# The end of a two-layer graph network on one core: another order of work for the last pair, written out on three engines

## The chip, the core and the metric

The kernel runs on one core of a Trainium2 chip. The core has a matrix engine (TensorE, PE in the profile, with its weight loads as PEld), a vector engine (VectorE, DVE), an activation engine (ScalarE, ACT), GpSimd (POOL) and SyncE (SP). Each engine runs its own queue of instructions in order, and the queues meet through semaphores. Matrix products go to PSUM, eight banks of 128 x 512 float32, and are read from there by ACT or DVE. Data comes from and goes to the device's memory (HBM) by DMA, issued here from the queues of SP and POOL.

The metric is the device time in microseconds (us), the median of several executions. Before the change it is 2423.75 us (three runs, 2422.8 to 2425.18).

## The reference

Input x has 64 batch elements of 256 nodes and 512 features; adj is a 0/1 matrix of 256 x 256. All is float32.

```python
q, k, v = ((x @ W + b) for W, b in ((Wq, bq), (Wk, bk), (Wv, bv)))    # 8 heads of 64
scores  = q @ k.T / sqrt(64) + (1 - adj) * -1e9
out     = softmax(scores) @ v @ Wo + bo
x       = layernorm(x + out)                         # layer 0
x       = layernorm(x + (adj @ x) @ weight + bias)   # layer 1
```

## The kernel before

**Pairs.** Batch elements are worked on two at a time: pair p of 32 has elements b = 0 and 1, each with two chunks of 128 nodes. Attention is done in two halves of four heads, g = 0 and 1 ("first" and "second" scores and values). The last pair is 31 (p in the code), the one before it 30 (q).

**Products.** Every large product runs as three float32r matmuls on digits of both factors: a high part (a scaled copy on ACT), a low part and a difference (two scalar_tensor_tensor on DVE, lines 268 and 269; for q and k lines 350 to 354). `product` (line 312) is one *block*: 12 matmuls of 128 x 512 (line 318) into one PSUM bank, then one evacuation. Blocks are named by their weights: "v", "q", "k", "o" (attention's output) and "l" (layer 1); four of each per pair, j = 2b + c. Digits of activations live in a pool of four buffers per name: "sh", "sl", "sd" or "high", "low", "diff". Blocks "o" and "l" are evacuated by DVE (line 325), which adds the residual r and sums each row.

**Attention.** `scores` (line 402) takes eight banks in a row and gives 48 matmuls (line 415) and eight exps on ACT (line 419) into the tiles e. `masked` multiplies e by the transposed adjacency matrix, `summed` adds the two halves of the keys (lines 424, 429, DVE). `values` (line 363) forms the sums by 16 matmuls (line 371), copied to zc by ACT (line 373), and the values by 64 small matmuls (line 381), copied to vc (line 385). DVE inverts the sums and multiplies (lines 388 to 400): O. `o_high` and `o_rest` make O's digits.

**Norms.** `with_bo` and `with_b1` add a bias to r (DVE, line 438). A norm over two chunks is `mean` (DVE, line 450), `squared` for each chunk (ACT, line 457, with the sum of squares), `inverse` (DVE line 462, then a pow on POOL, line 463), `less` (DVE, line 468) and `normed` for each chunk (ACT, line 474). After the second layer `normed` also issues the output's DMA on SP; for pair 31 that is one DMA for each chunk (line 477). `normed` of chunk 3 issues the load of r two pairs on (`load_r`, line 82), which waits until the output of the pair that held the buffer is written.

**Layer 1.** `hl_high` (ACT, line 486) and `hl_low` (DVE, line 491) split the normed x, `adj_x` (line 493) multiplies by the adjacency matrix (8 matmuls, line 501) and makes the digits of the result (ACT, then DVE).

**Order.** Functions are called in the order in which their instructions stand on PE, DVE and ACT: `first(w)` and `second(w)` do one pair's attention together with the layers of the pair before (`with tc.manual_schedule`, line 614). For the end, `last()` (line 583), only TensorE's order is as written (line 623); there the order on DVE and ACT comes from a scheduler. POOL and SP are the scheduler's in both. Weights pass through a ring of two stages of three tiles; `stage_end` issues the load of the stage after next on POOL's queue. Weights "o" and "l" of pair 30 stay in the ring for pair 31.

## Time and profile before

| | |
|---|---|
| median of the runs | 2423.75 us |
| profiled execution | 2424.03 us, its span 2422.3 us |
| one pair in the steady part | 73.8 us |
| pair 30's last o block ends | 2342.4 us |
| last matmul of a block ends | 2410.8 us |
| last norm on ACT ends | 2416.25 us |

Times in the tables of the profile are from the span's start. A row of the timeline has the start, the duration from the first start to the last end, the engine, the source line, the operation, what it writes and reads, the shapes and how many instructions it stands for; in brackets, if the engine was idle before, how long and what released it. A row of the table of stages has the stretch, its length, then for PE, PEld, DVE, ACT and POOL the busy time and the number of instructions, the clock granted to TensorE (1.00 is full speed), the share of the DMA engines' time and GB/s. The chain that ended last is followed back from the last instruction to what released each step.

### The profile page before, as it was taken

Reading aid. Unit: us, or ns where it says so; the run is one execution under the profiler, and the core shown is the slowest. Engines: PE = TensorE matmul, PEld = TensorE weight load, DVE = VectorE, ACT = ScalarE, POOL = GpSimd, SP = SyncE. Lnnn points to the kernel's source line nnn. Section 1 sums busy time; section 2 is a strip of 40 time slices with the busy share of each in tenths; the row PEclk is TensorE's granted clock in tenths of the full one; section 3 lists DMA queues with packets and bytes.
Section 4 is the critical chain, followed back from the end, with each engine's and each line's share of the span. In section 5 each row is a group of like instructions: output and inputs, shape, how many; then the busy total and the mean of one; then the engine's idle time right before and its main releaser. Section 6 shows DMA issues by size and latency. Waiting matters only on the chain.

```text
span 2422.3 us, 42885 instructions
## 1 busy us (share of the span) xinstructions
PE 2388.0 (99%) x16894; PEld 1914.0 (79%) x16894; DVE 2002.6 (83%) x3311; ACT 1503.2 (62%) x2796; POOL 448.8 (19%) x735
## 2 busy tenths in 40 slices
PE   8999999999999999999999999999999999999997
PEld 5778878888878888788888788887788787888876
DVE  7888888888888888888988888888889888888865
ACT  5566665665665666656656656666566566566554
POOL 1111121122121211211121212212111112112110
PEclk9999999999999999999999999999999999999998
DMA  8767787777897787877778977778877779777651
GB/s 260 269 221 268 256 278 260 239 239 260 254 306 242 227 268 256 266 270 243 235 261 251 305 249 225 261 258 261 281 239 237 264 251 293 255 229 252 247 191 37
DMA packets 370719, 603.45 MB, mean 249 GB/s; under 512 B 272848, under 2 KB 275152, under 8 KB 310224
## 3 DMA queue, kind: packets, MB, share of 16 engines
q0 software_dynamic: 67824, 493.91, 55.3%
q1 hardware_dynamic: 300576, 104.64, 20.2%
q8 instruction: 135, 2.21, 0.4%
q10 hardware_dynamic: 2112, 2.10, 0.2%
q14 instruction: 72, 0.59, 0.1%
HBM read 551.29 MB, written 49.28 MB: 248 GB/s over the span
## 4 chain that ended last, share of the span: by engine, by line
PE 91%; DVE 3%; ACT 1%; DMA 1%; issue 0%; POOL 0%; POOLq 0%; DVEq 0%; ACTq 0%; SPq 0%
PE ps L318 68%; PE ps L381 8%; PE ps L415 7%; PE ps L501 5%; PE ps L371 2%; DMA r<-in_x_dram 1%; ACT r L474 0%; DVE e L424 0%; DVE hl L491 0%; DVE wr L128 0%; ACT waste L457 0%; DVE sl L268 0%; DVE wr L127 0%; DVE r L438 0%; DVE r L325 0%
## 5 line engine op out<-in xcount | busy, mean ns | idle before, releaser
L424 DVE TENSOR_TENSOR e<-e,adjT 128x1024 f32<-128x1024 f32 x256 | 304.5, 1221 | 1.2 <-ACT e L419 1.2
L318 PE MATMUL ps<-wr,sl 128*128 128x512 f32 x1024 | 278.0, 393 | 6.2 <-ACT wr L131 3.9
L318 PE MATMUL ps<-wr,sh 128*128 128x512 f32 x1024 | 276.3, 391 | 0.0
L318 PE MATMUL ps<-wr,sd 128*128 128x512 f32 x1024 | 275.6, 391 | 0.0
L318 PE MATMUL ps<-low,wr 128*128 128x512 f32 x992 | 271.4, 395 | 0.0
L318 PE MATMUL ps<-high,wr 128*128 128x512 f32 x992 | 266.5, 390 | 0.0
L318 PE MATMUL ps<-diff,wr 128*128 128x512 f32 x992 | 265.0, 389 | 0.0
L419 ACT ACTIVATE e<-ps 128x512 f32<-128x512 f32 x512 | 256.8, 628 | 8.1 <-PE ps L415 8.1
L457 ACT ACTIVATE waste<-r,ln 128x512 bf16<-128x512 f32 x256 | 183.9, 719 | 106.4 <-DVE ln L450 104.2
L381 PE MATMUL ps<-e,v 128*32 128x256 f32 x4096 | 232.9, 379 | 1.2 <-ACT v L329 1.2
L474 ACT ACTIVATE r<-r,ln 128x512 f32<-128x512 f32 x256 | 194.8, 808 | 58.3 <-DMA x<-in_x_dram 31.4
L463 POOL TENSOR_TENSOR ln<-ln,power 128x2 f32<-128x2 f32 x128 | 152.3, 1190 | 412.4 <-DVE ln L462 353.8
L318 PEld LDWEIGHTS ps<-wr,sl 128*128 128x128 f32 x1024 | 191.2, 189 | 46.4 <-ACT wr L131 4.7
L318 PEld LDWEIGHTS ps<-wr,sh 128*128 128x128 f32 x1024 | 193.7, 189 | 41.0
L318 PEld LDWEIGHTS ps<-wr,sd 128*128 128x128 f32 x1024 | 193.3, 189 | 40.6
L318 PEld LDWEIGHTS ps<-high,wr 128*128 128x128 f32 x992 | 186.2, 188 | 41.1
L318 PEld LDWEIGHTS ps<-diff,wr 128*128 128x128 f32 x992 | 186.2, 188 | 39.1
L415 PEld LDWEIGHTS ps<-qT,kT 64*128 64x128 f32 x3056 | 188.9, 188 | 31.4 <-ACT vc L385 14.8
L338 ACT ACTIVATE uncut<-ps,bq 128x512 f32<-128x512 f32 x126 | 86.8, 689 | 199.7 <-PE ps L318 142.9
L350 DVE SCALAR_TENSOR_TENSOR qT<-qT,uncut 128x512 fp32r<-128x512 f32 x126 | 86.7, 688 | 148.2 <-ACT qT L343 148.2
L415 PE MATMUL ps<-qT,kT 64*128 64x256 f32 x3056 | 203.6, 286 | 3.9 <-ACT vc L385 3.1
L318 PEld LDWEIGHTS ps<-low,wr 128*128 128x128 f32 x992 | 177.9, 188 | 35.1 <-issue 0.5
(111 smaller groups left out, 4212.1 us busy)
## 6 DMA issues: line engine op xcount, KB each, us to landing
wr<-qk POOLq DMA_DIRECT2D x183, 1024.0 KB, 7.5
wr<-v POOLq DMA_DIRECT2D x93, 1024.0 KB, 6.7
wr<-o POOLq DMA_DIRECT2D x90, 1024.0 KB, 8.1
wr<-l POOLq DMA_DIRECT2D x90, 1024.0 KB, 8.4
r<-in_x_dram SPq DMA_DIRECT2D x32, 1024.0 KB
out_dram<-r SPq DMA_DIRECT2D x62, 512.0 KB
x<-in_x_dram SPq DMA_DIRECT2D x488, 64.0 KB
qk<-wr POOLq DMA_DIRECT2D x6, 1024.0 KB, 8.4
```

What stands on the lines that cost most here:

```text
L318: nc.tensor.matmul(pm, *pairs[k][i], start=i == 0 and k == 0, stop=i == n - 1 and k == DC - 1)
L338: nc.scalar.activation(to, pm, AF.Identity, bias=bias[:, j:j + 1], scale=scale)
L350: nc.vector.scalar_tensor_tensor(low, high.bitcast(F32), -RHO, UNCUT.pop((name, p, j)), op0=OP.mult, op1=OP.add)
L371: nc.tensor.matmul(at[h * 32:(h + 1) * 32, b, :], ones, sm[:, h % 2, h // 2, :], start=True, stop=True)
L381: nc.tensor.matmul(at[h * 32:(h + 1) * 32, a, :], V[p, b][:, kc, col:col + 32], E[p, g, b, kc][:, h % 2, h // 2, :], start=kc == 0, stop=k ...
L415: nc.tensor.matmul(sc[s][:, a, :], K[p, g][r, a, i, keys], Q[p, g][r, a, i, b * N:(b + 1) * N], start=i == digits[0], stop=i == digits[-1])
L419: nc.scalar.activation(e[:, s], sc[s], AF.Exp, scale=(RHO if (p, g) != (0, 0) else 1.0) * qscale)
L424: nc.vector.tensor_tensor(e, e, mask[:, kc:kc + 1, :].to_broadcast([P, 4, N]), op=OP.mult)
L457: nc.scalar.activation(waste, R[p][b][:, c], AF.Square, bias=t[0][:, c:c + 1], accum_out=t[1][:, c:c + 1])
L463: nc.gpsimd.tensor_tensor(t[2], t[1], power, op=OP.pow)
L474: nc.scalar.activation(r, r, AF.Identity, scale=t[2][:, c:c + 1], bias=t[3][:, c:c + 1])
L501: nc.tensor.matmul(pm[:, j, :], t[:, i, mc, j * P:(j + 1) * P], adjT[:, mc, :], start=mc == 0 and i == 0, stop=mc == NC - 1 and i == 1)
```

## The change

`last()` and the last call of `first` are replaced by `ending()`, which writes the order of pair 31's part on PE, DVE and ACT.

- The second scores of pair 31 no longer stand directly behind its first values, but two o blocks of pair 30 later. Attention of pair 31 stands ahead of the rest of pair 30's layer 1 and of pair 31's o blocks.
- The bias of pair 31's r is added (`with_bo`) behind the digits of the "k" blocks.
- For the second scores of pair 31 each e is two tiles of half the size, in buffers that x and the digits of x had ("x", "high", "low", "diff"); mask and sum work on the halves, each as two instructions in place of one. O of the second half goes to "xT". All digits of pair 31's activations go to "high", "low", "diff".
- `mean`, `inverse` and `less` take a range of chunks. The last norm is done chunk by chunk, so that each of its chunks is squared, inverted and normed by itself.

The computation and the number of matmuls are the same. The order of POOL's and SP's transfers is the same; on POOL there is one pow more.

```diff
--- before.py
+++ after.py
@@ -276,8 +276,7 @@
 
     def set_high(name, p, b, half, a):
 
-        free = p == NP - 1 and (name, half) != ("o", 0) and (name, b) != ("l", 1)
-        names = ("high", "low", "diff") if free else ("sh", "sl", "sd")
+        names = ("high", "low", "diff") if p == NP - 1 else ("sh", "sl", "sd")
         t = SET[name, p, b, half] = [four.tile([P, 2, N], F32R, name=n) for n in names]
         nc.scalar.activation(t[0], a, AF.Copy, scale=CUT)
 
@@ -379,7 +378,7 @@
                     for h in range(4):
                         col = g * HF + h * HD + a * 32
                         nc.tensor.matmul(at[h * 32:(h + 1) * 32, a, :], V[p, b][:, kc, col:col + 32],
-                                         E[p, g, b, kc][:, h % 2, h // 2, :], start=kc == 0, stop=kc == NC - 1)
+                                         E[p, g, b, kc][0][h % 2][:, h // 2, :], start=kc == 0, stop=kc == NC - 1)
             do(between[b])
             vc.append(two.tile([P, 2, N], F32, name="vc"))
             nc.scalar.activation(vc[b], at, AF.Copy)
@@ -396,7 +395,7 @@
         total = acc.rearrange("p b j -> p (b j)")
         nc.gpsimd.tensor_tensor(total, total, seen, op=OP.add)
         for b in range(2):
-            O[p, b, g] = two.tile([P, 2, N], F32, name="o")
+            O[p, b, g] = two.tile([P, 2, N], F32, name="o" if (p, g) != (NP - 1, 1) else "xT")
             nc.vector.tensor_tensor(O[p, b, g], vc[b], rs[:, b, None].to_broadcast([P, 2, N]), op=OP.mult)
 
     def scores(p, g):
@@ -414,19 +413,32 @@
                             r = slice(s * HD, (s + 1) * HD)
                             nc.tensor.matmul(sc[s][:, a, :], K[p, g][r, a, i, keys], Q[p, g][r, a, i, b * N:(b + 1) * N],
                                              start=i == digits[0], stop=i == digits[-1])
-                e = E[p, g, b, kc] = one.tile([P, 2, 2, N], F32, name=f"e{2 * b + kc}")
+                if (p, g) == (NP - 1, 1):
+
+                    names = (("x", two), ("high", four), ("low", four), ("diff", four))
+                    name, pool_of = names[2 * b + kc]
+                    e = [pool_of.tile([P, 2, N], F32, name=name) for _ in range(2)]
+                    whole = []
+                else:
+                    e = one.tile([P, 2, 2, N], F32, name=f"e{2 * b + kc}")
+                    whole, e = [e.rearrange("p s a n -> p (s a) n")], [e[:, s] for s in range(2)]
+                E[p, g, b, kc] = e, whole
                 for s in range(2):
-                    nc.scalar.activation(e[:, s], sc[s], AF.Exp, scale=(RHO if (p, g) != (0, 0) else 1.0) * qscale)
+                    nc.scalar.activation(e[s], sc[s], AF.Exp, scale=(RHO if (p, g) != (0, 0) else 1.0) * qscale)
 
     def masked(p, g, b, kc):
         if 0 <= p < NP:
-            e = E[p, g, b, kc].rearrange("p s a n -> p (s a) n")
-            nc.vector.tensor_tensor(e, e, mask[:, kc:kc + 1, :].to_broadcast([P, 4, N]), op=OP.mult)
+            halves, whole = E[p, g, b, kc]
+            for e in whole or halves:
+                nc.vector.tensor_tensor(e, e, mask[:, kc:kc + 1, :].to_broadcast([P, e.shape[1], N]), op=OP.mult)
 
     def summed(p, g, b):
         if 0 <= p < NP:
             sm = SM[p, g, b] = two.tile([P, 2, 2, N], F32, name="sm")
-            nc.vector.tensor_tensor(sm, E[p, g, b, 0], E[p, g, b, 1], op=OP.add)
+            (h0, w0), (h1, w1) = (E[p, g, b, kc] for kc in range(NC))
+            to = [sm.rearrange("p s a n -> p (s a) n")] if w0 else [sm[:, s] for s in range(2)]
+            for t, e0, e1 in zip(to, w0 or h0, w1 or h1):
+                nc.vector.tensor_tensor(t, e0, e1, op=OP.add)
 
     def masks(p, g, b):
         return [(masked, p, g, b, 0), (masked, p, g, b, 1), (summed, p, g, b)]
@@ -443,11 +455,12 @@
     def with_b1(p, b):
         biased(p, b, b1_s)
 
-    def mean(p, name, b):
-        if 0 <= p < NP:
-            ln = small.tile([P, 4, 2], F32, name="ln")
-            t = LN[p, name, b] = [ln[:, i] for i in range(4)]
-            nc.vector.tensor_scalar(t[0], ST.pop((p, name, b)), -1 / D, None, op0=OP.mult)
+    def mean(p, name, b, cs=slice(0, 2)):
+        if 0 <= p < NP:
+            if cs.start == 0:
+                ln = small.tile([P, 4, 2], F32, name="ln")
+                LN[p, name, b] = [ln[:, i] for i in range(4)]
+            nc.vector.tensor_scalar(LN[p, name, b][0][:, cs], ST[p, name, b][:, cs], -1 / D, None, op0=OP.mult)
 
     def squared(p, name, j):
         if 0 <= p < NP:
@@ -456,15 +469,15 @@
             waste = one.tile([P, D], mybir.dt.bfloat16, name="waste")
             nc.scalar.activation(waste, R[p][b][:, c], AF.Square, bias=t[0][:, c:c + 1], accum_out=t[1][:, c:c + 1])
 
-    def inverse(p, name, b):
-        if 0 <= p < NP:
-            t = LN[p, name, b]
+    def inverse(p, name, b, cs=slice(0, 2)):
+        if 0 <= p < NP:
+            t = [u[:, cs] for u in LN[p, name, b]]
             nc.vector.tensor_scalar(t[1], t[1], 1 / D, EPS, op0=OP.mult, op1=OP.add)
-            nc.gpsimd.tensor_tensor(t[2], t[1], power, op=OP.pow)
-
-    def less(p, name, b):
-        if 0 <= p < NP:
-            t = LN[p, name, b]
+            nc.gpsimd.tensor_tensor(t[2], t[1], power[:, cs], op=OP.pow)
+
+    def less(p, name, b, cs=slice(0, 2)):
+        if 0 <= p < NP:
+            t = [u[:, cs] for u in LN[p, name, b]]
             nc.vector.tensor_tensor(t[3], t[0], t[2], op=OP.mult)
 
     def normed(p, name, j):
@@ -580,35 +593,49 @@
            (block, "q", 1, 1), (k_low, 1, 0), qk0[4:6], (o_high, 0, 0, 0), (o_high, 0, 1, 0), (o_rest, 0, 0, 0),
            (block, "k", 1, 1), qk0[6:], (stage_end, 0), (k_low, 1, 1), (o_rest, 0, 1, 0))
 
-    def last():
+    def ending():
 
         p, q = NP - 1, NP - 2
-        values(p, 0, ([(squared, q, "o", 2), (hl_low, q, 0, 0), (hl_low, q, 0, 1)], [(squared, q, "o", 3)]))
+        c0, c1 = slice(0, 1), slice(1, 2)
+        values(q, 1, ([(squared, q - 1, "l", 2)], [(squared, q - 1, "l", 3)]))
+        scores(p, 0)
+        do((inverse, q - 1, "l", 1), masks(p, 0, 0),
+           (o_high, q, 0, 1), (o_high, q, 1, 1), (block, "v", p, 0), (o_rest, q, 0, 1), (o_rest, q, 1, 1),
+           (less, q - 1, "l", 1), masks(p, 0, 1), (normed, q - 1, "l", 0), (normed, q - 1, "l", 1),
+           (block, "v", p, 1), (normed, q - 1, "l", 2), (normed, q - 1, "l", 3),
+           (with_bo, q, 0), (with_bo, q, 1),
+           (block, "v", p, 2), (block, "v", p, 3), (stage_end, p),
+           (block, "q", p, 2), (qk_high, "q", p, 2), (qk_rest, "q", p, 2),
+           (block, "k", p, 2), (qk_high, "k", p, 2), (qk_rest, "k", p, 2), (with_bo, p, 0),
+           (block, "q", p, 3), (k_low, p, 2), (qk_high, "q", p, 3), (qk_rest, "q", p, 3),
+           (block, "k", p, 3), (stage_end, p), (qk_high, "k", p, 3), (qk_rest, "k", p, 3), (k_low, p, 3), (with_bo, p, 1))
+        values(p, 0)
+        do((block, "o", q, 0), (o_high, p, 0, 0), (o_high, p, 1, 0),
+           (block, "o", q, 1), (mean, q, "o", 0), (squared, q, "o", 0), (squared, q, "o", 1), (inverse, q, "o", 0))
         scores(p, 1)
-        do((inverse, q, "o", 1), (with_b1, q, 0), (less, q, "o", 1),
-           (normed, q, "o", 2), (normed, q, "o", 3), (adj_x, q, 0, 0), (adj_x, q, 0, 1),
-           masks(p, 1, 0), (hl_high, q, 1, 0), (hl_high, q, 1, 1), (hl_low, q, 1, 0), (hl_low, q, 1, 1), (with_b1, q, 1),
-           (block, "l", q, 0), masks(p, 1, 1), (block, "l", q, 1),
-           (adj_x, q, 1, 0), (adj_x, q, 1, 1),
-           (mean, q, "l", 0), (squared, q, "l", 0), (squared, q, "l", 1), (inverse, q, "l", 0),
-           (o_high, p, 0, 0), (o_rest, p, 0, 0), (o_high, p, 1, 0), (o_rest, p, 1, 0))
-        values(p, 1)
-        do((less, q, "l", 0), (o_high, p, 0, 1), (o_rest, p, 0, 1), (o_high, p, 1, 1), (o_rest, p, 1, 1),
-           (block, "l", q, 2), (normed, q, "l", 0), (normed, q, "l", 1), (with_bo, p, 0),
-           (block, "o", p, 0), (with_bo, p, 1), (block, "o", p, 1), (mean, p, "o", 0), (squared, p, "o", 0), (squared, p, "o", 1),
-           (inverse, p, "o", 0), (less, p, "o", 0), (normed, p, "o", 0), (normed, p, "o", 1),
-           (block, "o", p, 2), (hl_high, p, 0, 0), (hl_high, p, 0, 1), (hl_low, p, 0, 0), (hl_low, p, 0, 1),
-           (block, "o", p, 3), (mean, p, "o", 1), (squared, p, "o", 2), (squared, p, "o", 3), (inverse, p, "o", 1), (less, p, "o", 1),
-           (normed, p, "o", 2), (normed, p, "o", 3),
-           (block, "l", q, 3), (mean, q, "l", 1), (adj_x, p, 0, 0), (adj_x, p, 0, 1),
-           (hl_high, p, 1, 0), (hl_high, p, 1, 1), (hl_low, p, 1, 0), (hl_low, p, 1, 1), (with_b1, p, 0), (with_b1, p, 1),
-           (squared, q, "l", 2), (squared, q, "l", 3), (inverse, q, "l", 1), (less, q, "l", 1),
-           (block, "l", p, 0), (adj_x, p, 1, 0), (adj_x, p, 1, 1), (block, "l", p, 1),
-           (normed, q, "l", 2), (normed, q, "l", 3),
-           (mean, p, "l", 0), (squared, p, "l", 0), (squared, p, "l", 1), (inverse, p, "l", 0), (less, p, "l", 0),
-           (block, "l", p, 2), (normed, p, "l", 0), (normed, p, "l", 1), (block, "l", p, 3), (mean, p, "l", 1),
-           (squared, p, "l", 2), (squared, p, "l", 3), (inverse, p, "l", 1), (less, p, "l", 1),
-           (normed, p, "l", 2), (normed, p, "l", 3))
+        do((less, q, "o", 0), masks(p, 1, 0), (normed, q, "o", 0), (normed, q, "o", 1), masks(p, 1, 1)[:1],
+           (block, "o", q, 2), (hl_high, q, 0, 0), (hl_high, q, 0, 1), (hl_low, q, 0, 0), (hl_low, q, 0, 1), masks(p, 1, 1)[1:],
+           (block, "o", q, 3), (stage_end, q), (mean, q, "o", 1), (squared, q, "o", 2), (squared, q, "o", 3),
+           (inverse, q, "o", 1), (adj_x, q, 0, 0), (less, q, "o", 1), (adj_x, q, 0, 1))
+        values(p, 1, ([(normed, q, "o", 2), (normed, q, "o", 3)], [(hl_high, q, 1, 0), (hl_high, q, 1, 1)]))
+        do((o_high, p, 0, 1), (o_high, p, 1, 1), (hl_low, q, 1, 0), (hl_low, q, 1, 1), (o_rest, p, 0, 1), (o_rest, p, 0, 0),
+           (with_b1, q, 0), (block, "l", q, 0), (block, "l", q, 1), (mean, q, "l", 0), (adj_x, q, 1, 0), (adj_x, q, 1, 1),
+           (squared, q, "l", 0), (squared, q, "l", 1), (inverse, q, "l", 0),
+           (block, "o", p, 0), (block, "o", p, 1), (mean, p, "o", 0), (squared, p, "o", 0), (squared, p, "o", 1),
+           (o_rest, p, 1, 1), (inverse, p, "o", 0), (o_rest, p, 1, 0), (less, p, "o", 0), (with_b1, q, 1),
+           (block, "l", q, 2), (normed, p, "o", 0), (normed, p, "o", 1), (hl_high, p, 0, 0), (hl_high, p, 0, 1),
+           (block, "o", p, 2), (hl_low, p, 0, 0), (hl_low, p, 0, 1), (less, q, "l", 0), (normed, q, "l", 0),
+           (block, "o", p, 3), (mean, p, "o", 1), (squared, p, "o", 2), (squared, p, "o", 3), (inverse, p, "o", 1),
+           (adj_x, p, 0, 0), (less, p, "o", 1), (adj_x, p, 0, 1), (normed, p, "o", 2), (normed, p, "o", 3),
+           (hl_high, p, 1, 0), (hl_high, p, 1, 1), (block, "l", q, 3), (hl_low, p, 1, 0), (hl_low, p, 1, 1), (mean, q, "l", 1), (with_b1, p, 0),
+           (block, "l", p, 0), (adj_x, p, 1, 0), (adj_x, p, 1, 1), (normed, q, "l", 1), (squared, q, "l", 2), (squared, q, "l", 3), (inverse, q, "l", 1),
+           (with_b1, p, 1),
+           (block, "l", p, 1), (mean, p, "l", 0), (less, q, "l", 1), (squared, p, "l", 0), (squared, p, "l", 1), (normed, q, "l", 2),
+           (inverse, p, "l", 0), (normed, q, "l", 3),
+           (block, "l", p, 2), (mean, p, "l", 1, c0), (less, p, "l", 0), (squared, p, "l", 2), (normed, p, "l", 0), (normed, p, "l", 1),
+           (inverse, p, "l", 1, c0),
+           (block, "l", p, 3), (mean, p, "l", 1, c1), (less, p, "l", 1, c0), (squared, p, "l", 3), (inverse, p, "l", 1, c1),
+           (normed, p, "l", 2), (less, p, "l", 1, c1), (normed, p, "l", 3))
 
     PE, DVE, ACT = mybir.EngineType.PE, mybir.EngineType.DVE, mybir.EngineType.Activation
     with tc.manual_schedule(engines={PE, DVE, ACT}):
@@ -616,12 +643,10 @@
         first(1, steps_of("o", 0))
         second(1, steps_of("l", 0))
         load_r(1)
-        for w in range(2, NP):
+        for w in range(2, NP - 1):
             first(w)
-            if w < NP - 1:
-                second(w)
-    with tc.manual_schedule(engines={PE}):
-        last()
+            second(w)
+        ending()
 
     good = one.tile([P, 2, N // 32], F32, name="z")
     nc.vector.tensor_scalar(good, acc, RANGE, None, op0=OP.is_le)
```

## The prediction

> **What bounds the kernel now.** I read the page first: span, busy shares, then the chain that ended last.
>
> ```profile
> span 2422.3 us, 42885 instructions
> PE 2388.0 (99%) x16894; PEld 1914.0 (79%) x16894; DVE 2002.6 (83%) x3311; ACT 1503.2 (62%) x2796; POOL 448.8 (19%) x735
> ...
> PE 91%; DVE 3%; ACT 1%; DMA 1%; issue 0%; POOL 0%; POOLq 0%; DVEq 0%; ACTq 0%; SPq 0%
> ```
>
> TensorE is the bound over the whole. In the chain in order of time a pair takes 2269.74 - 2195.92 = 73.8 us, with TensorE never waiting. The steady part is written as before, so only the end can move. The timeline of TensorE alone, from 2340 us on, shows where it waits there (last bracket: idle time and releaser):
>
> ```profile
> 2350.09 0.38 PE L415 MATMUL ps<-qT,kT 64*128 64x256 f32 x1 [0.74 <-ACT vc L385]
> 2352.84 1.65 PE L415 MATMUL ps<-qT,kT 64*128 64x256 f32 x11 [2.37 <-ACT vc L385]
> ...
> 2359.90 1.22 PE L318 MATMUL ps<-wr,sl 128*128 128x512 f32 x2 [1.70 <-DVE sl L268]
> 2361.70 1.22 PE L318 MATMUL ps<-wr,sl 128*128 128x512 f32 x2 [0.58 <-DVE sl L268]
> ...
> 2379.77 0.73 PE L318 MATMUL ps<-wr,low 128*128 128x512 f32 x2 [0.92 <-DVE low L268]
> ...
> 2396.03 0.73 PE L318 MATMUL ps<-wr,low 128*128 128x512 f32 x2 [0.94 <-DVE low L268]
> ...
> 2398.19 0.73 PE L318 MATMUL ps<-wr,low 128*128 128x512 f32 x2 [1.43 <-DVE low L268]
> ```
>
> These waits sum to 8.7 us. The first two are the second scores of pair 31, which stand directly behind its first values and want banks that ACT has not emptied. Then the table of stages (its PEclk is the granted clock):
>
> ```profile
> 2350.00:2353.00 3.00, 0.54 (x3) 0.34 (x3) 1.98 (x7) 1.54 (x4) 1.07 (x3) 0.93 0.00 0
> 2353.00:2356.00 3.00, 3.00 (x18) 2.78 (x19) 2.02 (x3) 3.00 (x7) 0.00 (x0) 0.50 0.00 0
> ...
> 2363.00:2366.00 3.00, 3.00 (x8) 2.35 (x8) 2.12 (x2) 0.00 (x0) 0.00 (x0) 0.50 0.00 0
> 2366.00:2369.00 3.00, 3.00 (x14) 2.39 (x14) 1.84 (x3) 0.00 (x0) 0.00 (x0) 0.96 0.00 0
> ```
>
> After 3.1 us idle within 3.5, the clock is at half for 13.3 us (2352.8 to 2366.1). Less the 2.3 idle in them, half of 11 is lost: 5.5 us. The 2.37 us idle within 3.1 at 2395 left it at 1.00.
>
> So of the 68.4 us from 2342.4 (end of pair 30's o blocks) to the last matmul at 2410.8, 14.2 are waits and half clock. The work itself: 12 blocks of 2.72 (12 matmuls; starts 2.72 apart), values twice 4.54, scores 3.07, eight adj_x at 0.99 = 52.7. Behind the last matmul:
>
> ```profile
> 2414.73 1.52 ACT L474 ACTIVATE r<-r,ln 128x512 f32<-128x512 f32 x2 [1.26 <-DVE ln L468]
> ```
>
> That ends at 2416.25, and the output's transfer takes 6.05 us more to the span's end.
>
> **The change part by part.** I walk the written order over three engines with starts taken apart: ACT exp 0.50, square with its read 0.85, norm 0.76 to 0.80, high copies 0.57 to 0.65; DVE 512-wide two-input 0.60 to 0.65, 1024-wide 1.2, an evacuation (L325) 0.65; handovers 0.03 between DVE and ACT, 0.24 behind TensorE. "v", "q", "k" blocks of pair 31 stay up to 2331.5.
>
> *Attention ahead of the rest.* The bias add of pair 31 moves behind the digits of k block 2. It waits for r in both kernels, landing at 2332.7 (chain: 12.41 from 2320.28). Behind it on DVE stand the digits of q3 and k3: 2334.0 to 2336.6, then ACT's k low to 2337.3, and behind that zc and both vc to 2339.0. Cover: TensorE does values(31,0) 2331.5 to 2336.05 and o blocks 0 and 1 of pair 30 to 2341.5. The scores start there, 4.2 us after k is ready; that slack is the price of a later r. O is out of DVE at 2340.9, the two evacuations at 2342.5. The scores' first banks are free by 2339 and the last pair of banks at 2342.5, wanted at 2343.8: the 3.1 us wait and its half clock go, 8.6 with the 5.5.
>
> *What is late next.* ACT does the two squares of pair 30 (to 2344.4) before the exps, so the first exp frees a bank at 2345.05 against 2344.56: 0.55 wait for o block 2. Exps end 2348.4, norms 2350, hl_high 2351.2. DVE runs 2345.5 to 2354.7 unbroken: 12 half masks and sums, two hl_low, an evacuation. hl_low is done at 2351.65 where o block 3 ended 2350.55: 1.15 wait. The sums of the mask end 2354.7 where adj_x ended 2353.65: 1.1. Then values to 2359.2; l block 0 waits 0.4 for its second low (ACT's squares to 2357.35 hold back adj_x's copies, and DVE waits with them).
>
> *Behind the second values.* DVE is unbroken 2357.9 to 2372.8: O to 2363.85, hl_low 2365.1, o_rest of b0 2367.6, bias 2368.75, evacuations, rests. TensorE runs l 0, 1, adj_x, o31 0, 1, l 2 without wait to 2375.15. o31 block 2 needs o_rest(31,1,0), written behind the norm's inverse, which waits for squares ending 2376.1: low at 2376.9, a wait of 1.85. o31 3 ends 2382.45, adj_x 2384.4, l30 3 2387.15, l31 0 waits 0.45 (rest at 2388), adj_x, l31 1 2394.95, l31 2 2397.7, l31 3 2400.4.
>
> *The sum on TensorE.* 2342.4 + 52.7 + waits 5.5 (0.55 + 1.15 + 1.1 + 0.4 + 1.85 + 0.45) = 2400.6, the walk says 2400.4: 10.4 us sooner.
>
> *Norms by chunk.* Removed: one square and one norm behind the last evacuation, 0.85 + 0.76. Added: one mean, inverse, less on DVE (0.17 each), one pow on POOL. But ACT comes to the end late: with_b1 and a DVE wait for the squares of l30 put l31 1's evacuation at 2397.6, its squares at 2397.85 to 2399.55, pair 30's last norms to 2401.1, chunk 0's mean waits for those, square 2402.25, two norms 2403.8, square of chunk 1 2404.7, pow 2405.65, norm 2405.9 to 2406.7. So the tail from the last matmul is 6.3 instead of 5.5: 0.8 is given back. A pow of one column is in no row: between 0.22 (add of 16 columns, L395) and 1.59; I take 0.69, the commonest row of the same operation.
>
> *At nothing.* Halved masks: 12 halves are 7.2 to 7.7 against six whole at 1.2 = 7.2; I take 7.2, upper end +0.5. The exps' new tiles last held x and x's digits, read until 2331.5, ten us before. SP issues the same transfers in the same order, POOL's weight loads keep their places; the last outputs (1.5 MB from 2401.1 to 2406.7) would need 270 GB/s where the page's slices reach 320: 0 to +0.5.
>
> [...] POOL's pow took 0.69 with DVE idle and 1.59 at 2400.16 with the bias add (1.23) beside it. The written order puts DVE work beside most of the last pows, but there the less has 0.6 to 1.2 of other DVE work ahead of it. [...]
>
> Span: 2422.3 - 10.4 + 0.8 = 2412.7. The profiled execution took 2424.03, 1.73 outside its span and 0.28 above the runs' median of 2423.75: 2412.7 + 1.73 - 0.28 = 2414.2, 0.4% faster.
>
> **The rivals.**
>
> *The clock gate trips.* TensorE's waits of 1.15 and 1.1 stand 1.95 us apart; at most 1.55 idle fall in any 3.5 us, where 2.37 did nothing and 3.1 did. Against it stands that margin, for it that hand-walked waits grow. Price: 4.4 us at half (the recovery at 2361.7 to 2366.1 took that) costs 2.2, a full 13 us costs 5.5: 2416.4 to 2419.7. [...]
>
> *Better: the waits don't come.* Without them the last matmul is at 2395.1, and with 9.9 of tail (11.5 less 1.6) the time is 2406.5. Against: DVE has some 51 us of work in the 61 between O and the last evacuation, and each wait above has a named DVE or ACT item.
>
> *Slower: the squares stand in the path.* DVE and ACT now keep a written order, so at each of the eight norms from 2342 on what is behind the pair of squares waits out 1.73 us (rows of L462: idle 1.73, releaser ACT waste). If nothing hid them, that is 13.8 us; the walk charges TensorE 0.55, 0.4, 1.85 and 0.45 of it. The other 10.6 would give 2424.8, slower than before by 1; past 2428.6 only with half a us more behind each. It decides from 9.6 us of added wait. For it: DVE has 51 us of work (16 evacuations, 12 mask halves and sums, 8 hl_low, 8 rests of adj_x, 4 of o, 4 biases, two O, the small steps) in the 63.5 from 2339.6 to 2403.1. Against: at pair 30's l norms and the first o norm of 31, other DVE work is written into the wait.
>
> **How the numbers follow.** The walk, within 3 to 4 us of its sum: 0.68. Clock gate: 0.13. Better: 0.04. Squares in the path, with most of the gain gone: 0.09 inside 0.2% of before, 0.06 slower. About 0.2% (4.8 us) is what a measurement tells from no change; the limit is 2418.9, which about a sixth of the gate's case exceeds (0.02). Faster 0.68 + 0.11 + 0.04 = 0.83, same 0.09 + 0.02 = 0.11, slower 0.06. Range: the walk's 2410.5 below, and above to 2420.5 to take in the gate's 5.5 and the ends of the unknown costs (0.5 + 0.5 + 0.9).
>
> **What would show it.** Right: scores(31,1) without a wait at their start, granted clock 1.00 through 2350 to 2400, last matmul near 2400, o31 block 2 waiting some 2 us for DVE low, last norm at 2406 to 2407. Wrong: clock at 0.50 near 2355, an ACT wait at the first scores (r landing late), or a tail over 13 us.

## The result, and the profile after

The changed kernel takes 2413.28 us (median of five runs, 2412.33 to 2414.19), against 2422.95 us for the kernel before on the same chip (five runs, three of them those of the section on the time before). The ratio is 0.9957, 95% interval 0.9946 to 0.9968: 0.4% faster, 9.7 us. The prediction was 2414.2. Three of the later kernels (the second scores back, the second values late, the l blocks early) each had one slow execution of 3994 to 13675 us, which the ratios leave out and which moves their medians by 0.2 us at most.

The profiled execution took 2412.73 us, its span is 2411.0. From the page of the changed kernel, the span, the busy shares and the shares of the chain that ended last:

```profile
span 2411.0 us, 42905 instructions
PE 2382.0 (99%) x16894; PEld 1908.6 (79%) x16894; DVE 2003.9 (83%) x3320; ACT 1504.1 (62%) x2796; POOL 449.5 (19%) x736
...
PE 91%; DVE 3%; ACT 1%; DMA 1%; issue 0%; POOL 0%; POOLq 0%; DVEq 0%; ACTq 0%; SPq 0%
```

The matmuls are the same 16894 and TensorE is still the bound; its busy time fell by 6.0 us, about what the half clock cost, and the rest of the gain is idle time. Single profiles differ by up to 1.8 us in when the end of the kernel is reached (pair 30's second sums start between 2300.84 and 2302.67 in all the profiles of this study, whatever the end looks like). So I compare ends by their **length**: from the start of those sums to the matmul that counts, the last one on TensorE. Before: 2410.77 - 2302.09 = 108.68 us. After: 2399.94 - 2301.16 = 98.78. The change shortens it by 9.9; another 0.93 of the 11.3 between the two spans lies ahead of the change.

The timeline of TensorE in the changed kernel, with the rows that answer to those of before: the second scores, every wait, the sums of the second values, and the count.

```profile
2330.67 1.07 PE L370 MATMUL ps<-sm,ones 128*32 128x256 f32 x16
...
2340.83 3.14 PE L414 MATMUL ps<-qT,kT 64*128 64x256 f32 x48
2344.29 1.20 PE L317 MATMUL ps<-wr,sl 128*128 128x512 f32 x4 [0.32 <-ACT x L427]
...
2351.03 1.99 PE L514 MATMUL ps<-adjT,hl 128*128 128x256 f32 x15 [0.87 <-DVE hl L504]
2352.95 1.50 PE L370 MATMUL ps<-sm,ones 128*32 128x256 f32 x13
...
2359.14 0.73 PE L317 MATMUL ps<-wr,sl 128*128 128x512 f32 x2 [0.35 <-DVE sl L268]
...
2376.38 1.17 PE L317 MATMUL ps<-wr,low 128*128 128x512 f32 x4 [1.72 <-DVE low L268]
...
2387.37 0.73 PE L317 MATMUL ps<-wr,low 128*128 128x512 f32 x2 [0.20 <-DVE low L268]
...
2399.94 0.22 PE L656 MATMUL ps<-table,ones 128*32 128x1 f32 x2
```

The scores run without a wait. The waits in brackets sum to 3.46 us, where before had 8.68. One more is not in brackets: 13 of the sums take 1.50 us where 16 took 1.07 at 2330.67, and sums and values together take 5.10 (2352.95 to 2358.05) where the first ones took 4.45 (2330.67 to 2335.12). That is the wait for the mask's sums, about 0.6. The table of stages (after the busy times, the granted clock of TensorE) for the two longest waits:

```profile
2350.00:2353.00 3.00, 2.13 (x21) 1.85 (x23) 3.00 (x7) 0.24 (x1) 0.00 (x0) 1.00 0.03 5
2353.00:2356.00 3.00, 3.00 (x47) 1.44 (x50) 1.76 (x5) 1.14 (x3) 0.00 (x0) 1.00 0.00 0
...
2373.00:2376.00 3.00, 1.66 (x8) 1.04 (x6) 2.47 (x7) 1.63 (x4) 0.34 (x2) 1.00 0.00 0
2376.00:2379.00 3.00, 2.62 (x12) 2.20 (x13) 2.83 (x6) 1.91 (x3) 0.78 (x1) 1.00 0.00 0
```

The granted clock is 1.00 from 2325 us to 2404.58, 4.6 us behind the last matmul. The end on ScalarE:

```profile
2402.60 0.71 ACT L470 ACTIVATE waste<-r,ln 128x512 bf16<-128x512 f32 x1
...
2403.30 0.80 ACT L487 ACTIVATE r<-r,ln 128x512 f32<-128x512 f32 x1
2404.51 0.81 ACT L487 ACTIVATE r<-r,ln 128x512 f32<-128x512 f32 x1 [0.40 <-DVE ln L481]
```

The last norm ends at 2405.32, 5.4 us behind the last matmul (5.5 before), and the output takes 5.7 us more (6.05 before).

### The profile page after: what moved, and what is told of

Its sections match the earlier page's. It is cut to its first block, busy times and chain, and to the rows that moved or that the text cites. A ratio compares the mean times of both kernels' runs of the same rounds, so it can differ in the third digit from the quotient of the medians.

```text
span 2411.0 us, 42905 instructions
## 1 busy us (share of the span) xinstructions
PE 2382.0 (99%) x16894; PEld 1908.6 (79%) x16894; DVE 2003.9 (83%) x3320; ACT 1504.1 (62%) x2796; POOL 449.5 (19%) x736
## 4 chain that ended last, share of the span: by engine, by line
PE 91%; DVE 3%; ACT 1%; DMA 1%; issue 0%; POOL 0%; POOLq 0%; DVEq 0%; ACTq 0%; SPq 0%
PE ps L317 68%; PE ps L380 8%; PE ps L414 8%; PE ps L514 5%; PE ps L370 2%; DMA r<-in_x_dram 1%; ACT r L487 0%; ACT waste L470 0%; DVE r L324 0%; DVE wr L128 0%; DVE hl L504 0%; DVE low L268 0%; DVE wr L127 0%; DVE sm L441 0%; DVE r L450 0%
## 5 line engine op out<-in xcount | busy, mean ns | idle before, releaser
L317 PE MATMUL ps<-wr,sl 128*128 128x512 f32 x1008 | 271.6, 391 | 4.6 <-ACT wr L131 3.9
L317 PE MATMUL ps<-wr,sh 128*128 128x512 f32 x1008 | 270.6, 390 | 0.0
L317 PE MATMUL ps<-wr,sd 128*128 128x512 f32 x1008 | 269.7, 389 | 0.0
L414 PEld LDWEIGHTS ps<-qT,kT 64*128 64x128 f32 x3056 | 188.1, 187 | 27.8 <-PE ps L380 12.3
L114 POOL DMA_DIRECT2D wr<-qk x183 | 98.5, 539 | 564.4 <-PE ps L317 564.3
```

The costliest lines, as they stand in the source:

```text
L114: nc.gpsimd.dma_start(W[stage][i], SCRATCH[name, i])
L317: nc.tensor.matmul(pm, *pairs[k][i], start=i == 0 and k == 0, stop=i == n - 1 and k == DC - 1)
L414: nc.tensor.matmul(sc[s][:, a, :], K[p, g][r, a, i, keys], Q[p, g][r, a, i, b * N:(b + 1) * N], start=i == digits[0], stop=i == digits[-1])
```

## The experiments

The result fits the prediction's total, but does not yet show its reason: that the wait at the second scores and the half clock behind it (8.6 us) go. The first four kernels take the parts of the change one at a time; the later ones follow what these showed. Every kernel was timed in five rounds beside the kernel before, whose medians were 2424.23 (first four), 2423.9 (next four) and 2424.01 (last four).

### The order behind the first values on TensorE alone

```diff
+    def ending_rest():      # all of ending() from values(p, 0) on
...
     with tc.manual_schedule(engines={PE, DVE, ACT}):
         ending()
+    with tc.manual_schedule(engines={PE}):
+        ending_rest()
```

> From the first values of pair 31 on, only TensorE's order is as written; the order on VectorE and ScalarE is the scheduler's, as before the change. Theory P (the gain comes from where the second scores stand on TensorE: two o blocks behind the values, so that banks are empty in time and the clock stays whole): no wait at the scores, clock 1.00, time 2412 to 2416. Rival W (the gain comes from the order written on VectorE and ScalarE): the scheduler again puts squares and norms ahead of what TensorE waits for, waits of 2 us or more on TensorE, time 2418 or more.

2414.28 us, ratio 0.9963 (0.9949 to 0.9976); length 100.98. Two of its waits, from its timeline of TensorE:

```profile
2351.85 1.99 PE L514 MATMUL ps<-adjT,hl 128*128 128x256 f32 x15 [1.96 <-DVE hl L504]
...
2389.83 0.38 PE L514 MATMUL ps<-adjT,hl 128*128 128x256 f32 x1 [1.44 <-ACT hl L499]
```

The scheduler does the second hl_low 1.1 us later than the written order, and the clock is at half from 2391.05 to 2394.46 (behind a window with 1.78 us idle, as the last section counts it), yet the time is within 1 us of the changed kernel's, as theory P expected. By length the end is 2.2 us longer. So writing the order on VectorE and ScalarE behind this point carries a small part of the gain at most.

### The second scores back at their first values

```diff
         values(p, 0)
+        scores(p, 1)
         do((block, "o", q, 0), ...
-        scores(p, 1)
```

> The changed kernel with the second scores of pair 31 directly behind its first values on TensorE, as before; everything else in the written order. Theory P: the scores again stand before banks that are not empty, 3 us idle and half clock, time 2418 to 2422. Rival W: with zc and both vc written ahead of the squares on ScalarE the scores wait only for the digits of k (about 1.3 us, no half clock) and the exps come sooner, so 2410 to 2415.

2417.21 us, ratio 0.9971 (0.996 to 0.9982); length 102.88. TensorE's timeline:

```profile
2336.20 2.78 PE L414 MATMUL ps<-qT,kT 64*128 64x256 f32 x42 [0.78 <-ACT kT L358]
...
2354.57 3.57 PE L514 MATMUL ps<-adjT,hl 128*128 128x256 f32 x15 [3.43 <-DVE hl L504]
```

Neither expectation holds. The place costs 3.9 us when it is undone, not 8.6, and not at the scores: there the wait is 0.78, for the k digits. The o blocks 0 and 1 of pair 30 come 3 us later, their norm and its parts with them, and the first adj_x waits 3.43 in its midst, with the clock at half from 2353.0 to 2359.8.

### The last norm over both chunks at once

```diff
-           (block, "l", p, 2), (mean, p, "l", 1, c0), ...
+           (block, "l", p, 2), (less, p, "l", 0), (normed, p, "l", 0), (normed, p, "l", 1),
+           (block, "l", p, 3), (mean, p, "l", 1), (squared, p, "l", 2), (squared, p, "l", 3), (inverse, p, "l", 1), ...
```

> The changed kernel with the last norm of pair 31 over both chunks at once, as before. If the norm by chunk is worth what its removed square and norm say, less what late ScalarE work takes back: 0.5 to 1.0 us later, 2413.8 to 2414.3, with the last norm 0.8 later behind the last matmul than in the changed kernel. Rival (the chunk's extra pow and steps eat it): within 0.3 us.

2413.04 us, ratio 0.9955 (0.9941 to 0.9969): no difference, as the rival said. Its timeline of ScalarE at the end:

```profile
2404.59 1.52 ACT L487 ACTIVATE r<-r,ln 128x512 f32<-128x512 f32 x2 [1.27 <-DVE ln L481]
```

That ends at 2406.11, 5.95 us behind its count at 2400.16, so chunks do bring the last norm 0.6 us forward. But here the output takes 5.0 us to the span's end and with chunks 5.7: in these two profiles the transfer takes back what the chunks gain.

### The order of before, written on three engines

```diff
-    with tc.manual_schedule(engines={PE}):
+    with tc.manual_schedule(engines={PE, DVE, ACT}):
         last()
```

> The kernel before, with its own old order of the end now holding on VectorE and ScalarE too; nothing is moved on TensorE. Theory P: the scores stand where they stood, so wait and half clock stay, 2420 or more. Rival W: ScalarE does zc, square, vc, square, vc and then the exps, as in the steady part where TensorE never waits; the 3.1 us wait and the half clock go, 8.6 us, and the old order's later waits (0.92, 0.94, 1.43) stay or grow: 2414 to 2418.

2429.05 us, ratio 1.0022 (1.0013 to 1.0031), slower; length 113.69. TensorE's timeline:

```profile
2346.83 3.14 PE L415 MATMUL ps<-qT,kT 64*128 64x256 f32 x48
...
2354.51 1.00 PE L318 MATMUL ps<-wr,sl 128*128 128x512 f32 x2 [2.46 <-DVE sl L268]
...
2378.87 1.22 PE L318 MATMUL ps<-wr,low 128*128 128x512 f32 x2 [4.67 <-DVE low L268]
...
2399.50 2.55 PE L318 MATMUL ps<-wr,low 128*128 128x512 f32 x4 [3.80 <-DVE low L268]
```

The wait at the second scores, the one the prediction removed, is gone altogether, and the kernel is 4.8 us slower: 13.2 us of waits stand elsewhere, in front of steps that need VectorE's digits or sums. Neither expectation holds: theory P kept the wait, and rival W had a gain.

### The second scores moved, and nothing else

The kernel before, with the first values of pair 31 ahead of pair 30's o blocks and the second scores two blocks behind, the rest in the old order. With the move, the work of these o blocks on VectorE and ScalarE falls to the scheduler too.

```diff
-        values(p, 0, ([(squared, q, "o", 2), (hl_low, q, 0, 0), (hl_low, q, 0, 1)], [(squared, q, "o", 3)]))
+        values(p, 0)
+        do((block, "o", q, 0), (block, "o", q, 1), (mean, q, "o", 0), ..., (inverse, q, "o", 0))
         scores(p, 1)
+        do((block, "o", q, 2), (less, q, "o", 0), ..., (block, "o", q, 3), (mean, q, "o", 1), ...)
         do((inverse, q, "o", 1), (with_b1, q, 0), ...
```

> The kernel before, with one move on TensorE: pair 31's first values ahead of pair 30's o blocks and its second scores two o blocks behind them; the rest of TensorE's order is the old one, VectorE and ScalarE are ordered by the scheduler. Theory P (this move is the gain: 3.1 us of wait and 5.5 us of half clock): no wait of over 0.6 us at the scores, 2415 to 2419. Rival Q (the other moves, the second values ahead of pair 30's l blocks and the l blocks as filler, carry as much; the wait only moves to the first l block or to the second values): 2419 to 2423.

2422.86 us, ratio 0.9995 (0.9986 to 1.0004): no gain, as rival Q said; length 107.26. Its timeline of TensorE and two of its stages:

```profile
2344.99 0.98 PE L415 MATMUL ps<-qT,kT 64*128 64x256 f32 x11 [0.16 <-DVE r L325]
...
2355.30 3.53 PE L501 MATMUL ps<-adjT,hl 128*128 128x256 f32 x15 [2.22 <-DVE hl L491]
...
2377.39 0.73 PE L318 MATMUL ps<-wr,low 128*128 128x512 f32 x2 [2.00 <-DVE low L268]
```

```profile
2356.00:2359.00 3.00, 2.83 (x14) 2.53 (x12) 3.00 (x6) 0.73 (x2) 0.00 (x0) 0.53 0.00 0
...
2398.00:2400.00 2.00, 2.00 (x7) 1.55 (x7) 1.00 (x2) 0.39 (x1) 1.38 (x1) 0.56 0.00 0
```

Again the wait at the scores is gone (0.16 us), and 8.4 us of waits are still there, with the clock at half twice, for 3.4 us each. So the named wait was where VectorE's and ScalarE's lateness was met first, not what made them late.

### Pair 31's last operand ahead of the norm's inverse

```diff
-           (o_rest, p, 1, 1), (inverse, p, "o", 0), (o_rest, p, 1, 0), (less, p, "o", 0), ...
+           (o_rest, p, 1, 1), (o_rest, p, 1, 0), (inverse, p, "o", 0), (less, p, "o", 0), ...
```

> The changed kernel with one swap on VectorE: the digits of pair 31's O, element 1, first half, are made ahead of the inverse of the first norm instead of behind it. By the trace of the changed kernel VectorE has 0.46 us of idle there and the low digits would be ready 0.8 us sooner: TensorE's wait of 1.72 falls to about 0.9, time 2412.5. Rival (what follows is set by VectorE and ScalarE, so a shorter wait of TensorE comes back as another): same as the changed kernel, 2413.3, with TensorE's waits behind it grown by 0.8.

2413.28 us, ratio 0.9955 (0.9941 to 0.9969); length 97.96.

```profile
2377.06 1.17 PE L317 MATMUL ps<-wr,low 128*128 128x512 f32 x4 [1.10 <-DVE low L268]
```

The wait at o block 2 of pair 31 falls from 1.72 to 1.10, no later wait grows, and the end gets 0.8 shorter; in the time that cannot be told. It shows that the largest wait left has the cause that the prediction gave it: those digits stand behind the inverse, which waits for ScalarE's squares.

### Extra work on ScalarE ahead of the second exps

```diff
+        for _ in range(3):        # and, in a second kernel, 6
+            nc.scalar.activation(one.tile([P, D], mybir.dt.bfloat16, name="waste"), bo_s, AF.Copy)
         scores(p, 1)
```

> The changed kernel with three extra copies of 128x512 on ScalarE (some 0.55 us each) ahead of pair 31's second exps, so that o block 2 waits for its bank about 2 us instead of 0.32. Both theories: at most 1.7 us later than the changed kernel, 2413.5 to 2415. If less than 3 us of idle trips no gate, the clock stays 1.00.

> The same with six copies: o block 2 waits about 3.6 us. Theory G (a wait of that size costs its length and then a stretch at half clock, as at the scores of the kernel before): clock 0.50 behind the wait, half of the stretch's 3.4 to 7 us more, 2418 to 2420. Rival (the half clock costs nothing, since VectorE and ScalarE set the pace there): only the 1.7 us of three more copies above the run with three, 2415 to 2416.7.

2415.27 and 2417.43 us, 2.0 and 4.15 above the changed kernel; ratios 0.9964 (0.995 to 0.9978) and 0.9977 (0.9967 to 0.9988); lengths 100.02 and 102.68, 1.2 and 3.9 more. The timeline of TensorE with three copies, and its stages:

```profile
2345.99 1.73 PE L317 MATMUL ps<-wr,sl 128*128 128x512 f32 x4 [2.09 <-ACT x L427]
```

```profile
2344.00:2346.00 2.00, 0.01 (x1) 0.01 (x1) 0.19 (x2) 1.94 (x5) 0.46 (x1) 1.00 0.00 0
2346.00:2348.00 2.00, 2.00 (x6) 1.56 (x7) 2.00 (x4) 2.00 (x5) 0.00 (x0) 0.60 0.00 0
2348.00:2350.00 2.00, 2.00 (x7) 1.57 (x6) 2.00 (x4) 2.00 (x5) 0.00 (x0) 0.54 0.00 0
2350.00:2352.00 2.00, 2.00 (x10) 1.66 (x9) 2.00 (x5) 1.90 (x4) 0.00 (x0) 1.00 0.00 0
```

The three copies cost a little more than the 1.7 expected, and the time with six lies between theory G and its rival. With three copies, and a wait of 2.09, the clock is at half already, for 3.4 us (2346.42 to 2349.83); with six the wait is 4.07 and the clock is at half for 6.8 (2346.88 to 2353.71). Yet the time rises by about the wait alone (1.77 and 3.75 more of it). TensorE at half clock comes later to the first adj_x, where VectorE's parts then lie ready: that wait (0.87) and the one at l block 0 (0.35) are gone in both. The last four runs ask which parts carry the gain.

### The old order on TensorE behind the scores

The kernel with the order on TensorE alone, but behind the second scores with the order of the kernel that moved only these. Against that kernel it has the rest of the change: own tiles and halved masks for the last exps, all digits in the freed buffers, and the new order ahead of the first values.

> The changed kernel's buffers, halved exps and masks, and its order up to the first values of pair 31; behind the second scores TensorE has the old order (second values behind the l blocks 0 and 1 of pair 30 and both adj_x, l blocks 2 and 3 of pair 30 ahead of pair 31's o blocks and of its adj_x), and VectorE and ScalarE are left to the scheduler there. Theory T (the new places on TensorE behind the scores carry the 8.6 us between the order written on TensorE alone, 2414.3, and the move of the scores alone, 2422.9): 2421 to 2424, with waits of 2 us and more at adj_x of pair 30 and at an o block of pair 31, and a halved clock behind them. Rival B (the own buffers of the last exps, their halved masks and the order ahead of the scores carry it): 2413 to 2417.

2417.07 us, ratio 0.9972 (0.9962 to 0.9982); length 103.75. Neither expectation holds: it lies between. By medians, 5.8 of the 8.6 us come with the tiles and the order ahead (3.5 by the lengths), 2.8 with TensorE's order behind the scores (2.8 by both). The first step stands clear of its interval, the second does not. What the first half does can be read on VectorE. The kernel before, the one that moved only the scores, and this one, in that order, at the load of pair 31's r:

```profile
2332.81 2.36 DVE L438 TENSOR_TENSOR r<-r,bo 128x1024 f32<-128x1024 f32 x2 [6.46 <-DMA r<-in_x_dram]
2335.08 0.69 DVE L350 SCALAR_TENSOR_TENSOR kT<-kT,uncut 128x512 fp32r<-128x512 f32 x1
```

```profile
2333.29 2.36 DVE L438 TENSOR_TENSOR r<-r,bo 128x1024 f32<-128x1024 f32 x2 [6.40 <-DMA r<-in_x_dram]
2335.57 0.68 DVE L350 SCALAR_TENSOR_TENSOR kT<-kT,uncut 128x512 fp32r<-128x512 f32 x1
...
2342.42 1.29 DVE L400 TENSOR_TENSOR o<-vc,zc 128x512 f32<-128x512 f32 x2
```

```profile
2327.56 0.69 DVE L353 SCALAR_TENSOR_TENSOR kT<-kT 128x512 fp32r<-128x512 f32 x1
2332.10 1.22 DVE L450 TENSOR_TENSOR r<-r,bo 128x1024 f32<-128x1024 f32 x1 [3.84 <-DMA r<-in_x_dram]
2333.24 0.68 DVE L349 SCALAR_TENSOR_TENSOR qT<-qT,uncut 128x512 fp32r<-128x512 f32 x1
...
2338.60 1.29 DVE L399 TENSOR_TENSOR o<-vc,zc 128x512 f32<-128x512 f32 x2
```

And the first sums of pair 31 in the last two:

```profile
2332.13 1.07 PE L371 MATMUL ps<-sm,ones 128*32 128x256 f32 x16
```

```profile
2330.78 1.07 PE L370 MATMUL ps<-sm,ones 128*32 128x256 f32 x16
```

In the first two kernels the digits of k block 2 stand behind both bias adds, and these behind the load of r: VectorE idles 6.4 us, the last five of them with these digits' input ready (in the kernel before, ScalarE has written it by 2327.62). Where the bias add is written behind the digits of k block 2 (2327.56), and its second half apart, O comes 7.8 us behind the first sums (2338.60 - 2330.78) instead of 10.3 (2342.42 - 2332.13), 2.5 us sooner, and what VectorE does next comes sooner too: the inverse of pair 30's first norm stands 13.2 us behind the sums instead of 15.1 (2344.02 and 2347.20). This is a reading of the rows. How much of the 5.8 is this and how much the halved masks was not separated; the kernel before with only its bias adds moved was not run.

### The second values late

The kernel with the order on TensorE alone, with the second values behind pair 30's l blocks 0 and 1 and its second adj_x.

```diff
-        values(p, 1, ([(normed, q, "o", 2), ...], [(hl_high, q, 1, 0), ...]))
-        do(..., (block, "l", q, 0), (block, "l", q, 1), (mean, q, "l", 0), (adj_x, q, 1, 0), (adj_x, q, 1, 1),
+        do(..., (block, "l", q, 0), (block, "l", q, 1), (mean, q, "l", 0), (adj_x, q, 1, 0), (adj_x, q, 1, 1))
+        values(p, 1)
+        do((o_high, p, 0, 1), (o_high, p, 1, 1), ...
```

> The kernel whose ending is written on TensorE alone (2414.3), with the second values of pair 31 moved back behind l blocks 0 and 1 and the second adj_x of pair 30; all else as there. Theory V (the 5 us of sums and values are the cover of pair 30's last norm chain, and their place carries most of the gain): adj_x of pair 30's second half starts about 5 us earlier and waits 2 us or more for its high and low parts, the clock halves behind it, 2417 to 2421. Rival F (the l blocks that stand between pair 31's steps carry it): 2413 to 2416, no wait above 1 us between 2353 and 2368.

2420.77 us, ratio 0.9987 (0.9979 to 0.9996); length 107.18: 6.5 us lost by medians. TensorE's timeline:

```profile
2356.40 1.52 PE L317 MATMUL ps<-wr,sl 128*128 128x512 f32 x4 [2.24 <-DVE sl L268]
...
2374.70 2.04 PE L317 MATMUL ps<-wr,low 128*128 128x512 f32 x4 [4.48 <-DVE low L268]
```

The place of the values counts, but not as expected at the second adj_x. l block 0 waits for the digits of the first adj_x, which the values had covered, and o block 0 of pair 31 waits 4.48 us for the digits of the attention just computed, which l 0, l 1 and adj_x had covered. The values and these blocks are each other's cover; the old order avoided the second wait by another l block in between (no wait there in the experiment above).

### The l blocks of pair 30 early

The same kernel, with only l block 2 of pair 30 ahead of pair 31's o blocks and l block 3 ahead of both adj_x, where before had them.

> The kernel whose ending is written on TensorE alone (2414.3), with l block 2 of pair 30 ahead of pair 31's o blocks and l block 3 of pair 30 ahead of both adj_x of pair 31, where the kernel before has them. Rival F (the l blocks' places carry the gain): the first adj_x of pair 31 has 2.7 us less cover from block 2 and as much more from block 3, the second has 2.7 us less and waits 3 to 4 us in place of 1.44 + 0.34, with a halved clock behind it: 2417 to 2420. Theory V (the second values' place carries it): 2413 to 2416.

2414.62 us, ratio 0.9958 (0.9945 to 0.9971): no difference from 2414.28. The waits change places (2.47 at l block 2, which then comes too soon behind its adj_x), and the time stays. That is what theory V expected.

### Exps ahead of the squares

A version to beat the changed kernel: the first four second exps ahead of the two squares of pair 30's norm on ScalarE, their masks ahead of the inverse on VectorE (idle 1.73 and 0.82 us there, for squares and pow), and the swap of the operand above.

```diff
-           (block, "o", q, 1), (mean, q, "o", 0), (squared, q, "o", 0), (squared, q, "o", 1), (inverse, q, "o", 0))
-        scores(p, 1)
-        do((less, q, "o", 0), masks(p, 1, 0), ...
+           (block, "o", q, 1), (mean, q, "o", 0))
+        scores(p, 1, [(squared, q, "o", 0), (squared, q, "o", 1)])     # behind the exps of b = 0
+        do(masks(p, 1, 0)[:2], (inverse, q, "o", 0), masks(p, 1, 0)[2:], (less, q, "o", 0), ...
```

> The changed kernel with the two squares of pair 30's first norm behind the first four of the eight second exps, the masks of these ahead of the norm's inverse on VectorE, and pair 31's last operand parts ahead of the next inverse. If the rest of the waits are what the walk says (0.32 at o block 2, 0.87 at the first adj_x, 1.72 at o block 2 of pair 31): the first goes, the second falls to about 0.3, the third to 1.1, together 1.3 to 1.5, so 2411.5 to 2412.3. Rival (a step behind takes it back: the norm's high and low parts come no earlier, since ScalarE still does its norms behind all eight exps): the wait at adj_x stays 0.8 to 1.5 and the time 2412.8 to 2414.

2412.4 us (2411.91 to 2412.68), ratio 0.9952 (0.9939 to 0.9965); length 97.39. That is between the two expectations. TensorE's timeline:

```profile
2351.38 1.99 PE L516 MATMUL ps<-adjT,hl 128*128 128x256 f32 x15 [0.34 <-DVE hl L506]
...
2376.12 1.17 PE L317 MATMUL ps<-wr,low 128*128 128x512 f32 x4 [1.10 <-DVE low L268]
```

The waits are as first expected: the one at o block 2 is gone, the others are 0.34 and 1.10. The end is 1.4 us shorter than the changed kernel's; the median is 0.9 lower, less than the intervals can tell.

## Why the prediction was right, and where it was not

The sum came out: -9.6 us predicted, -9.7 measured; the last matmul was put at 2400.4, and as the steady part of this profile ran 0.93 sooner that means 2399.5, against 2399.94. That the two figures agree to 0.1 is partly luck. The waits came 1.4 shorter than walked, the walk left out some 1.5 of gaps, and the tail came 1.2 shorter. And the base of the comparison, 2422.95, is 0.8 under the one that the forecast started from; against the later medians of the kernel before (2423.9 to 2424.23) the gain is 10.6 to 11. Point by point:

- **The wait at the second scores and its half clock (8.6).** Both went, as walked. As a cause it does not stand by itself: two kernels lost that wait and gained nothing or lost 4.8 us, and putting the scores back cost 3.9, through adj_x. What made the 9.7 came in three steps: VectorE's and ScalarE's work sooner (k digits out from behind the bias adds, with the own tiles and halved masks; 5.8 by medians, 3.5 by lengths), other work of TensorE in front of each step that depends on them (2.8 by both), and the written order on the two engines (1.0 and 2.2). The intervals of the last two overlap with their neighbours'; together they are clear, since the slowest run of the changed kernel (2414.19) is below the fastest with the old order behind the scores (2415.36). Which of the parts in the first step carries it is not shown. The prediction walked the move of the bias adds and gave it no share of the gain. In TensorE's own account some 4.6 of the 9.9 are waits (8.7 before, 4.1 after) and the rest is about what the half clock cost.
- **The new waits (5.5).** All six stand where they were walked, and all are shorter: 0.32 for 0.55, 0.87 for 1.15, about 0.6 for 1.1, 0.35 for 0.4, 1.72 for 1.85, 0.20 for 0.45; together 4.1. The mis-sized term that offset this is in the sum: of before's 68.4 us, 52.7 work and 14.2 waits leave 1.5, which the sum for the new kernel left out. In part these are gaps where TensorE goes from one kind of work to another, and they are in the new kernel too: the sums start 1.00 us behind the last four matmuls of a block in both (2341.48 to 2342.48, 2329.67 to 2330.67), where within a block four matmuls start 0.91 behind the four before.
- **The tail (0.8 given back).** It gave back nothing: from the last matmul to the span's end 11.1 us against 11.5 before, where 12.3 were forecast. Pair 30's last norms were where the walk put them (2400.1, with the 0.93); behind them I added the square of chunk 1, its pow and its norm up to 0.45 us too long (the pow of one column took 0.55 where I took 0.69, the square starts in the norm's shadow), the last matmul was 0.47 later than walked, so that less of the tail lay behind it, and the output took 5.7 where I kept 6.05. (The page's slices reach 306 GB/s, not the 320 that I set against the output's 270.) That chunks shorten the norm's path was right (0.6); that they move the time was not.
- **The clock gate as a rival (0.13).** It did not trip, but the margin I gave was none: "2.37 did nothing and 3.1 did" is no threshold, as the last section shows (a wait of 2.09 was followed by a half clock). Nor was "at most 1.55 idle" true of my own walk, which had a wait of 1.85 in one piece. That wait came, and its window of the changed kernel (2373.86 to 2377.27) has 1.71 us idle, where the clock halved elsewhere behind 1.63 and 1.78; that it did not trip here is in part luck.
- **A half clock priced in full (2.2 to 5.5).** Not where a wait followed: with three copies the clock was at half for 3.4 us and the time rose by 2.0 (the length by 1.2), where the wait alone had grown by 1.77.
- **The pow beside VectorE (0.9).** No run shows the end later by the 0.9 us that the range takes in for it. A pow beside a bias add was long again (1.53 us at 2395.15, 1.59 in before), but the chunks' last pows did not meet such an instruction. One ran beside an evacuation (VectorE from 2401.39 to 2402.07) and took 0.55 at 2401.62, as long as the one with VectorE idle at 2403.67. In before, too, the pow of 0.69 at 2408.65 stands beside an evacuation, so "with DVE idle" was not the condition.
- **Squares in the path.** They cost no more than the walk charged. Where nothing covered them (2341.9 to 2344.8 on VectorE), covering them took 0.85 off the waits (0.32 and 0.53) and some 0.6 off the length (97.39 against 97.96 with the swap alone); in the time that cannot be told.

## What to carry to other kernels

A wait that the profile names is where a late engine was met first; before pricing its removal, walk on to the next step that needs the same engine, because the wait reappears there unless other work of TensorE stands in front of it or the late engine is really earlier. Look for what the late engine itself idles on: here 6.4 us on a load, for five of them with ready work queued behind it. And when a walk of the old kernel leaves a rest, carry the rest into the new sum.

## What the hardware showed

In every profile of this study in which the granted clock changes more than once from 2325 us on (before, and nine of the kernels above), the times between the changes are whole multiples of one length, 3.413 us (40.96 / 12 in what follows), to 0.03. In the kernel before the clock halves at 2352.58 and recovers at 2366.24 (13.66, 4 of them); with the scores moved alone the clock halves at 2355.39 and at 2396.35 (40.96, 12 of them) and recovers 3.41 later each time. So I divide each profile at its changes of the clock and at whole multiples of 3.413 us from them, and call the pieces windows. The kernel before, at the two waits 0.94 and 1.43 that left its clock at 1.00:

```profile
2393.54:2396.95 3.41, 2.29 (x16) 1.64 (x14) 2.41 (x8) 3.41 (x8) 0.69 (x1) 1.00 0.00 0
2396.95:2400.36 3.41, 2.17 (x9) 1.80 (x10) 2.92 (x6) 2.21 (x5) 0.20 (x1) 1.00 0.00 0
```

The same two waits in the kernel that moved only the scores:

```profile
2392.94:2396.35 3.41, 1.26 (x4) 0.78 (x5) 2.63 (x6) 3.41 (x8) 0.00 (x0) 1.00 0.00 0
2396.35:2399.76 3.41, 3.41 (x9) 2.65 (x9) 2.65 (x6) 0.59 (x3) 1.59 (x1) 0.50 0.00 0
```

In the first an edge falls between the waits, each window has 1.1 to 1.2 us idle (3.41 less TensorE's busy time, the first number), and the clock stays at 1.00; in the second both lie in one window, 2.15 idle, and from its end the clock is at 0.50. Divided in this way, from 2325 us on, all windows at full speed with 2.09 us idle or more were followed by a half clock, and none with 1.6 or less; between these both occur (1.63 and 1.78 were followed by it, 1.71 and 1.83 were not), with busy times that are partly modelled. The way back is less plain: a window at half clock with 0.32 us idle (the order of before on three engines, 2354.79 to 2358.20) was followed by full speed, but one of before with 0.26 (2352.58 to 2355.99) by half. Between the two kernels printed here, then, the same two waits differ in where the edges fall; what sets the edges was not shown. That this is why some kernels here spread by 3 to 5 us from run to run was not tested.
